# Cross-attention on one core: bias on ScalarE, V1 behind two energy tiles, second x behind y

## The chip, the cores and the metric

The kernel runs on one core of a Trainium2 chip. The metric is device time in microseconds (us), the median of several runs; lower is better. One further execution was taken by the hardware profiler, and all rows below come from it. Engines: TensorE (PE; its weight loads are PEld), VectorE (DVE), ScalarE (ACT), GpSimd (POOL) and SyncE (SP), which issues transfers.

## The reference

For each of 32 batches, x and y are 256 channels by 1024 positions (fp32), and the weights are 256 x 256:

```python
x_q = einsum('oc,bcn->bno', w_qk, y);  x_k = einsum('oc,bcn->bon', w_qk, x)
x_v = einsum('oc,bcn->bon', w_v, x) + b_v
attention = softmax(einsum('bnc,bcm->bnm', x_q, x_k), axis=-1)
attention = attention / (1e-07 + attention.sum(axis=1, keepdims=True))
x_r = einsum('bcn,bnm->bcm', x_v, attention)
return x + relu(einsum('oc,bcn->bon', w_t, x - x_r) + b_t)
```

## The kernel before

**Forms.** Each fp32 operand of a product is split into three forms (HIGH, REST, LOW), and a product is the sum of three products of forms. So every step of TensorE is 12 matmuls of 128x512 or a like number. The weights are multiplied together once: `gw` is w_qk's square, `vw` is w_t w_v, `tw` is w_t transposed. The bias of v goes through w_t as well: w_t times b_v is needed as `ubias` (times 1e-7), `nbias` (less b_t) and `xbias` (b_t less it).

**Tokens.** The order of TensorE is written out by hand in strings of tokens (lines 167 to 181): SET_UP, then FIRST for the first batch, STEADY for the next 29, BEFORE for the last but one and LAST for the last.

- `k0 k1`: keys, g = gw x, with the forms `gf` (one ScalarE operation and two VectorE operations of 1024 columns each).
- `V0 V1` (for the first batch's own, `v0` for the next batch's first half): values of one half of the positions (line 420). VectorE transposes PSUM into `turned`; four stores take `turned` to DRAM (`blocks`); one load brings it back, into `yr` for the first half and into `turned` for the second; ScalarE and GpSimd make the forms `uf`.
- `W0 W1`: w_t x, read from PSUM by ScalarE with `xbias` into `xe` (line 470).
- `E0`..`E7`: energy of 128 positions (line 478), then softmax: minimum on VectorE, exponential with its sum on ScalarE, reciprocal, and for each half of the columns VectorE's sum into `acc` and the forms `ef` (HIGH on ScalarE, REST on VectorE); LOW is made on ScalarE and GpSimd.
- `A0`..`A7` (in the last batch the eighth is cut into `a0 a1`): uf times ef, summed in PSUM over the eight. A0 to A3 need uf's first half, A4 to A7 the second.
- `S`: sums of attention over rows, on VectorE, giving `rc`. `O`: finish: (A + ubias) rc, plus xe, relu, plus x again, and the store. In the last batch `R`, `D`, `F`, `G` do this in another way: D1 divides in PSUM, F1 adds w_t x on top and stores, G0 does the other half of the channels.
- `X`: load the next batch's x and make its forms `xf` (line 359). `Y2 Y3`: load the next batch's y, one half of the positions each (line 327), into `yr` and then the forms `yf`; two of them are made by accumulating transfers on GpSimd's queue.
- In SET_UP `z` is a product of zeros that keeps TensorE busy, `G` and `H` are the halves of gw, `T` and `Q` the transposition of w_t and vw, `x0 x1` the forms of the first x, `fJkh` a piece of the first keys, `b` the bias (line 820), `y` both loads of the first y.

**PSUM.** There are four pairs of banks. A token with `^` takes turns on the pairs 3 and 2 (`upper`, line 863); the others take turns on 0 and 1. The A tokens sum in pairs 2 and 3. A token can start when the pair's earlier content has been read.

**The planner.** `Plan` (line 17) holds every operation with its engine, an assumed duration and lag, and the names it reads and writes. TensorE keeps the order of the tokens. The lists of the other engines, SP's and GpSimd's transfers among them, are made by list scheduling: of the operations that are ready, the one due first, where the due time is what its users leave less an optional `early`. The names only set the order; on the chip an operation waits for the data that it really touches.

The operations of the page all have line 231, the line of the helper that records them.

Of the kernel before, what the change touches and what calls it, by code (L numbers as in the profile page):

```python
# [9 lines left out]
F32 = mybir.dt.float32  # L10
F32R = mybir.dt.float32r
AF = mybir.ActivationFunctionType
ALU = mybir.AluOpType
AX = mybir.AxisListType


class Plan:
# [147 lines left out]


SET_UP = (
    "z z G H z x0 x1 fH00 z z z T fR00 b fL00 fH01 fR01 fL01 Q fH11 fR10 fL11 fL10 y fH10 fR11"
)
FIRST = (  # L170
    "V0^ V1^ W1^ E0 E1^ W0^ E2 X E3 A0 A1 E4 Y2 E5 A2 A3 E6 E7 A4 A5 S Y3 v0 A6 A7 O k0 k1"
)
STEADY = (
    "W0^ E0^ E1 E2 W1^ V1^ E3 Y2 A0 E4 A1 E5 A2 X E6 A3 E7 Y3 S A4 A5 v0 k1 A6 A7 k0 O"
)
BEFORE = (
    "V1^ E0 E1 W0^ W1^ E2 A0 E3 X A1 E4 A2 E5 A3 E6 Y2 E7 A4 Y3 A5 v0 k1 A6 k0 A7 S O"
)
LAST = (
    "E0 E1^ V1^ E2 E3 A0 A1 E4 E5 A2 A3 E6 E7 R1 A4 A5 S W0 A6 a0 a1 G0 D1 F1"  # L180
)


# [1 line left out]
def kernel(  # L185
# [13 lines left out]
    P = 128  # L199
    KC = C // P  # L200
# [4 lines left out]
    EPS = 1e-7  # L205
# [12 lines left out]
    one = ctx.enter_context(tc.tile_pool(name="one", bufs=1))  # L218
# [17 lines left out]
    pe, dve, act, pool, sync = (InOrder(g) for g in (nc.tensor, nc.vector, nc.scalar, nc.gpsimd, nc.sync))  # L236
    plan = Plan()


    def on_pe(count, columns, reads, writes, trace):  # L240
        plan.add("pe", count * max(columns / 2400 + 1 / 75, 1 / 9), 0.163, reads, writes, trace)

    def on_act(columns, reads, writes, trace, more=0.0):
        plan.add("act", columns / 1200 + 0.1 + more, 0.09, reads, writes, trace)

    def on_dve(columns, reads, writes, trace):
        plan.add("dve", columns / 960 + 0.16, 0.0, reads, writes, trace)

    def dve_in_sbuf(columns, reads, writes, trace):
        busy = columns / 960 + 0.07  # L250
# [5 lines left out]
    def on_pool(columns, reads, writes, trace):  # L256
        busy = columns * 2.25 / 1024 + 0.12
        plan.add("pool", busy, 0.0, reads, writes, trace, port=busy)

    def by_sync(landing, reads, writes, trace, early=0.0):  # L260
        plan.add("sync", 0.4, landing, reads, writes, trace, early=early)
# [4 lines left out]
    def by_pool(landing, reads, writes, trace):  # L266
        plan.add("pool", 1.2, landing, reads, writes, trace)

    def value(v):
        return v.bitcast(F32)  # L270

    def flat(p):
        return p.rearrange("p h m -> p (h m)")

    def accumulate(into, from_):
        pool.dma_start(into, from_, accum_op=ALU.add)
# [5 lines left out]
    ubias = const.tile([P, KC, 1], F32, name="ubias")  # L282
    xbias = const.tile([P, KC, 1], F32, name="xbias")
# [7 lines left out]
    xr = one.tile([P, KC, N], F32, name="xr")  # L291
    yr = one.tile([P, KC, MB], F32, name="yr")
    xo = one.tile([P, N], F32, name="xo")
    turned = one.tile([P, N], F32, name="turned")
    blocks = outside.tile([P, N], F32, name="blocks")
    xe = one.tile([P, KC, N], F32, name="xe")
    z = one.tile([P, KC, N], F32, name="z")
    acc = one.tile([P, N], F32, name="acc")
    rc = one.tile([P, N], F32, name="rc")
    small = one.tile([P, 3, NT, 1], F32, name="small")  # L300
    nbias = one.tile([P, KC, 1], F32, name="nbias")
    banks = ps_m.tile([P, 8, MB], F32, name="banks")

    def pair(j):
        return banks[:, 2 * j : 2 * j + 2]

    def in_pair(j):
        return [f"bank{2 * j}", f"bank{2 * j + 1}"]

    def matmul(into, lhs, rhs, start, stop):  # L310
        pe.matmul(into, lhs, rhs, start=start, stop=stop, skip_group_check=True)
# [44 lines left out]
    def x_names(j, k, halves=range(MH)):  # L356
        return [f"xf{j}{k}{h}" for h in halves]

    def load_x(b):
        for k in range(KC):  # L360

            def of(k=k):
                raw = [f"xr{k}{h}" for h in range(MH)]
                by_sync(5.0, [], raw, lambda: sync.dma_start(xr[:, k], x[b, ts(k, P)]))
                on_act(N, raw, x_names(HIGH, k), lambda: act.copy(xf[:, HIGH, k], xr[:, k]))
                on_pool(
                    N, raw + x_names(HIGH, k), x_names(REST, k),
                    lambda: pool.tensor_tensor(xf[:, REST, k], xr[:, k], value(xf[:, HIGH, k]), ALU.subtract),
                )
                on_act(  # L370
                    N, x_names(HIGH, k), x_names(LOW, k),
                    lambda: act.mul(xf[:, LOW, k], value(xf[:, HIGH, k]), 1.0 / UP),
                )
                by_pool(
                    8.2, x_names(LOW, k) + x_names(REST, k), x_names(LOW, k),
                    lambda: accumulate(value(xf[:, LOW, k]), value(xf[:, REST, k])),
                )

            of()
# [40 lines left out]
    def values(b, q, j_pair):  # L420

        both, at, u = pair(j_pair), in_pair(j_pair), uf[q]
        for i in range(KC):
            for j in ORDER:

                def of(i=i, j=j):
                    for k in range(KC):
                        matmul(
                            both[:, i], vw[:, j, k, ts(i, P)], xf[:, j, k, ts(q, MB)],
                            j == ORDER[0] and k == 0, j == ORDER[-1] and k == KC - 1,  # L430
                        )

                on_pe(KC, MB, [f"vw{j}{k}" for k in range(KC)] + [f"xf{j}{k}{q}" for k in range(KC)], [at[i]], of)
        on_dve(
            N, at, ["turned"],
            lambda: dve.transpose(
                turned.rearrange("p (a t i r) -> p i t a r", a=NG, t=HT, i=KC),
                both.rearrange("p i (t a r) -> p i t a r", t=HT, a=NG),
            ),
        )  # L440
        names = [f"uf{q}{j}" for j in range(FORMS)]

        def out_of():
            for g in range(NG):
                sync.dma_start(
                    blocks.rearrange("(a r) (g s) -> r g a s", a=NG, g=NG)[:, g],
                    turned[ts(g, G32)].rearrange("p (a s) -> p a s", a=NG),
                )

        plan.add("sync", 2.4, 3.0, ["turned"], ["blocks"], out_of)  # L450
        back, name = (turned, "turned") if q else (flat(yr), "yr")
        by_sync(4.5, ["blocks"], [name], lambda: sync.dma_start(back, blocks))

        def natural(v):
            return v.rearrange("p (t g s) -> p g t s", t=HT, g=NG)

        raw = back.rearrange("p (g t s) -> p g t s", t=HT, g=NG)
        high, low, rest = (natural(u[:, j]) for j in range(FORMS))
        on_act(N, [name], [names[HIGH]], lambda: act.copy(high, raw))
        on_pool(  # L460
            N, [name, names[HIGH]], [names[LOW]],
            lambda: pool.tensor_tensor(low, raw, value(high), ALU.subtract),
        )
        on_act(N, [names[LOW]], [names[LOW]], lambda: act.mul(u[:, LOW], value(u[:, LOW]), UP))
        on_pool(
            N, [name, names[LOW]], [names[REST]],
            lambda: pool.tensor_tensor(rest, raw, value(low), ALU.subtract),
        )
# [134 lines left out]
    def divided(c):  # L603

        for h in range(MH):

            def of(c=c, h=h):
                p = pair(2 + c)[:, h]
                on_dve(
                    MB, [in_pair(2 + c)[h], "rc", "bias"], [in_pair(2 + c)[h]],  # L610
                    lambda: dve.scalar_tensor_tensor(p, p, ubias[:, c], rc[:, ts(h, MB)], ALU.add, ALU.mult),
                )

            of()
# [69 lines left out]
    bt = two(3)[:, 0, P : P + KC].rearrange("p (k o) -> p k o", o=1)  # L684
# [135 lines left out]
    def biases():  # L820

        by_sync(5.6, [], ["bv"], lambda: sync.dma_start(bvs, b_v.partition_broadcast(P)), early=38.0)
        by_sync(
            5.4, [], ["bt"], lambda: sync.dma_start(bt, b_t.rearrange("(k p o) -> p k o", p=P, o=1)), early=36.0
        )
        each = two(0)
        on_pool(
            KC * C, ["wt0", "wt1", "bv", "z0", "z1"], ["wqk0", "wqk1"],
            lambda: pool.tensor_tensor(each, wt, bvs.unsqueeze(1).broadcast_to([P, KC, C]), ALU.mult),
        )  # L830

        def of():
            dve.tensor_reduce(nbias[:, :, 0], each, AX.X, ALU.add)
            dve.tensor_scalar(ubias[:, :, 0], nbias[:, :, 0], EPS, None, ALU.mult)
            dve.tensor_tensor(nbias[:, :, 0], nbias[:, :, 0], bt[:, :, 0], ALU.subtract)
            dve.tensor_scalar(xbias[:, :, 0], nbias[:, :, 0], -1.0, None, ALU.mult)

        plan.add("dve", 1.05, 0.0, ["wqk0", "wqk1", "bt", "z0", "z1"], ["bias"], of, port=1.05)

    def set_up(token):  # L840
        if token in ("G", "H"):
# [102 lines left out]
```

## Time and profile before

| | |
|---|---|
| median of 3 runs | 1937.35 us (1935.9 to 1937.73) |
| profiled execution | 1940.7 us, span of its instructions 1938.9 us |
| mean granted TensorE clock | 0.998 |
| TensorE matmul busy | 1928.4 us, 99% |
| TensorE weight load busy | 1595.3 us, 82% |
| VectorE, ScalarE, GpSimd busy | 77%, 76%, 80% |
| chain that ended last | TensorE 98%, VectorE 1% |

A row of a timeline has the start in us, the duration, the engine, the line, the operation, the tile written and those read, the shapes, and how many were merged; the bracket has the idle time of the engine ahead of it and what ended that. A row of windows has the stretch, its length, the busy time of PE, PEld, DVE, ACT and POOL with the number of instructions, the granted clock, the share of the DMA engines and GB/s. A row of groups has the count, then busy time, mean ns of one, and idle time ahead. Matmuls overlap in their records, so the pace is read from the starts.

### The profile page before, as it was taken

How to read it: one execution, taken by the hardware profiler on the slowest of the kernel's cores; microseconds unless marked ns; L12 is line 12 of the kernel's file. 1: busy time of each engine (PE TensorE's matmuls, PEld its weight loads, DVE VectorE, ACT ScalarE, POOL GpSimd, SP SyncE). 2: the span in 40 equal slices, each digit the busy share in tenths (PEclk: the TensorE clock that was granted, in tenths of full speed). 3: DMA queues.
4: the chain of work that ended last, by engine and by line, in shares of the span. 5: the costliest groups of instructions: out<-in, count | busy, mean ns of one | idle time of the engine just before them, and what ended most of it. 6: DMA issues, size and time to landing. Idle time of an engine off the chain costs nothing.

```text
span 1938.9 us, 24286 instructions
## 1 busy us (share of the span) xinstructions
PE 1928.4 (99%) x8494; PEld 1595.3 (82%) x8494; DVE 1499.1 (77%) x2109; ACT 1470.6 (76%) x1932; POOL 1553.9 (80%) x773
## 2 busy tenths in 40 slices
PE   8999999999999999999999999999999999999999
PEld 7888888888888888888888888888888888888887
DVE  6787777777777877778777787777787777877778
ACT  5779777787777877778877779777787777887776
POOL 4878878888778887788887878878888778887777
PEclk9999999999999999999999999999999999999999
DMA  6665666757666666666666665766756666666652
GB/s 182 142 162 153 178 154 137 166 153 181 162 143 151 159 170 168 147 145 168 163 165 155 147 163 152 181 156 138 164 151 178 163 145 149 161 170 169 156 106 76
DMA packets 128650, 301.88 MB, mean 156 GB/s; under 512 B 12688, under 2 KB 47120, under 8 KB 128528
## 3 DMA queue, kind: packets, MB, share of 16 engines
q1 hardware_dynamic: 92272, 200.45, 33.7%
q0 software_dynamic: 35680, 99.10, 29.0%
q8 instruction: 66, 1.08, 0.2%
q10 hardware_dynamic: 576, 0.79, 0.1%
q14 instruction: 56, 0.46, 0.1%
HBM read 167.38 MB, written 67.11 MB: 121 GB/s over the span
## 4 chain that ended last, share of the span: by engine, by line
PE 98%; DVE 1%; DMA 0%; ACT 0%; issue 0%; SPq 0%; DVEq 0%
PE banks L231 98%; DMA blocks<-turned 0%; DVE xf L231 0%; DVE nbias L231 0%; DVE z L231 0%; DVE turned L231 0%; DVE ef L231 0%; DVE parts L231 0%; DVE acc L231 0%; ACT ef L231 0%; DVE xbias L231 0%; DVE rc L231 0%; DVE banks L231 0%; DVE small L231 0%; SPq L231 0%
## 5 line engine op out<-in xcount | busy, mean ns | idle before, releaser
L231 PE MATMUL banks<-gf,yf 128*128 128x512 f32 x3072 | 729.6, 390 | 3.5 <-DVE turned L231 3.5
L231 POOL TENSOR_TENSOR ef<-ef 128x1024 fp32r<-128x1024 f32 x256 | 649.6, 2539 | 100.4 <-DVE acc L231 59.5
L231 PE MATMUL banks<-ef,uf 128*128 128x512 f32 x3072 | 727.0, 389 | 0.0
L231 PEld LDWEIGHTS banks<-gf,yf 128*128 128x128 f32 x3072 | 578.0, 188 | 124.3 <-DVE turned L231 3.9
L231 PEld LDWEIGHTS banks<-ef,uf 128*128 128x128 f32 x3072 | 576.6, 188 | 119.7
L231 DVE TENSOR_REDUCE small<-banks 128x1 f32<-128x1024 f32 x256 | 312.5, 1221 | 145.7 <-PE banks L231 145.7
L231 DVE SCALAR_TENSOR_TENSOR ef<-banks,small,ef 128x512 fp32r<-128x512 f32 x512 | 372.4, 743 | 56.5 <-ACT ef L231 55.4
L231 ACT ACTIVATE ef<-banks,small 128x512 fp32r<-128x512 f32 x512 | 336.4, 688 | 12.8 <-DVE acc L231 1.2
L231 ACT ACTIVATE banks<-banks,small 128x1024 f32<-128x1024 f32 x256 | 279.4, 1091 | 60.9 <-DVE small L231 60.6
L231 DVE SCALAR_TENSOR_TENSOR acc<-banks,small,acc 128x512 f32<-128x512 f32 x448 | 317.3, 744 | 5.6
L231 ACT ACTIVATE gf<-banks 128x1024 fp32r<-128x1024 f32 x64 | 65.8, 1030 | 315.9 <-PE banks L231 315.9
L231 ACT ACTIVATE ef<-ef 128x1024 fp32r<-128x1024 f32 x256 | 272.9, 1067 | 1.2
L231 POOL TENSOR_TENSOR z<-z,xe 128x1024 f32<-128x1024 f32 (+1 forms) x64 | 150.4, 2366 | 119.2 <-DVE z L231 116.8
L231 POOL TENSOR_TENSOR uf<-yr,uf 128x1024 fp32r<-128x1024 f32 x64 | 153.4, 2397 | 55.3 <-ACT uf L231 55.3
L231 PE MATMUL banks<-xf,tw 128*128 128x512 f32 x774 | 184.9, 388 | 2.1 <-DVE turned L231 1.2
L231 PE MATMUL banks<-xf,gw 128*128 128x512 f32 x768 | 185.3, 390 | 0.0
L231 PE MATMUL banks<-xf,vw 128*128 128x512 f32 x768 | 184.4, 389 | 0.0
L231 PEld LDWEIGHTS banks<-xf,tw 128*128 128x128 f32 x774 | 144.7, 188 | 32.9 <-DVE turned L231 1.6
L231 PEld LDWEIGHTS banks<-xf,vw 128*128 128x128 f32 x768 | 144.1, 188 | 30.2 <-DVE z L231 0.2
L231 PEld LDWEIGHTS banks<-xf,gw 128*128 128x128 f32 x768 | 143.8, 188 | 30.4 <-issue 0.4
L231 POOL TENSOR_TENSOR xf<-xr,xf 128x1024 fp32r<-128x1024 f32 x62 | 149.2, 2407 | 23.8 <-DVE turned L231 22.1
L231 POOL TENSOR_TENSOR uf<-turned,uf 128x1024 fp32r<-128x1024 f32 x64 | 156.2, 2441 | 0.3 <-ACT uf L231 0.3
(68 smaller groups left out, 1597.7 us busy)
## 6 DMA issues: line engine op xcount, KB each, us to landing
yr<-in_ctx_dram SPq DMA_DIRECT2D x64, 512.0 KB, 3.9
blocks<-turned SPq DMA_DIRECT2D x256, 128.0 KB, 3.0
yf<-in_ctx_dram POOLq DMA_DIRECT2D x63, 512.0 KB, 6.1
yf<-yf POOLq DMA_DIRECT2D x63, 512.0 KB, 7.1
xr<-in_x_dram SPq DMA_DIRECT2D x62, 512.0 KB, 3.6
xo<-in_x_dram SPq DMA_DIRECT2D x62, 512.0 KB, 4.4
xf<-xf POOLq DMA_DIRECT2D x62, 512.0 KB, 5.5
out_dram<-z SPq DMA_DIRECT2D x62, 512.0 KB, 4.5
```

Source lines behind the costliest of these rows:

```text
L231: self.last = getattr(self.engine, name)(*args, **kwargs)
```

## The change

The biases' reduction stays on VectorE, into a tile of its own; the three operations behind it become four on ScalarE. The token strings change except STEADY's, the planner is told of another lag for the first batch's stores to `blocks`, of an earlier due time for D's operations, and of a need of `yr` for the load of the second batch's x.

```diff
 SET_UP = (
-    "z z G H z x0 x1 fH00 z z z T fR00 b fL00 fH01 fR01 fL01 Q fH11 fR10 fL11 fL10 y fH10 fR11"
+    "x1 z z z G z x0 z H fH00 fH01 b z fR00 T fL00 fR01 Q fL01 fR11 fR10 fL11 fH11 y fH10 fL10"
 )
 FIRST = (
-    "V0^ V1^ W1^ E0 E1^ W0^ E2 X E3 A0 A1 E4 Y2 E5 A2 A3 E6 E7 A4 A5 S Y3 v0 A6 A7 O k0 k1"
+    "V0^ W1^ E0^ E1 V1^ E2^ W0^ E3 A0 X A1 E4 E5 A2 A3 Y2 E6 E7 Y3 A4 A5 k1 v0 A6 A7 S O k0"
 )
...
 BEFORE = (
-    "V1^ E0 E1 W0^ W1^ E2 A0 E3 X A1 E4 A2 E5 A3 E6 Y2 E7 A4 Y3 A5 v0 k1 A6 k0 A7 S O"
+    "V1^ E0 W0^ E1 W1^ X E2 A0 E3 A1 E4 A2 E5 A3 E6 E7 Y2 A4 Y3 A5 v0 k0 k1 A6 S A7 O"
 )
 LAST = (
-    "E0 E1^ V1^ E2 E3 A0 A1 E4 E5 A2 A3 E6 E7 R1 A4 A5 S W0 A6 a0 a1 G0 D1 F1"
+    "E0 E1^ V1^ E2 E3 A0 A1 E4 E5 A2 A3 E6 R1 E7 A4 A5 W0 A6 a0 S a1 D1 F1 G0"
 )
...
-    def on_dve(columns, reads, writes, trace):
-        plan.add("dve", columns / 960 + 0.16, 0.0, reads, writes, trace)
+    def on_dve(columns, reads, writes, trace, early=0.0):
+        plan.add("dve", columns / 960 + 0.16, 0.0, reads, writes, trace, early=early)
...
+    wtb = one.tile([P, KC, 1], F32, name="wtb")
...
-                by_sync(5.0, [], raw, lambda: sync.dma_start(xr[:, k], x[b, ts(k, P)]))
+                by_sync(5.0, ["yr"] if b == 1 else [], raw, lambda: sync.dma_start(xr[:, k], x[b, ts(k, P)]))
...
-        plan.add("sync", 2.4, 3.0, ["turned"], ["blocks"], out_of)
+        plan.add("sync", 2.4, 3.0 if b else 5.0, ["turned"], ["blocks"], out_of)
...
                     lambda: dve.scalar_tensor_tensor(p, p, ubias[:, c], rc[:, ts(h, MB)], ALU.add, ALU.mult),
+                    early=3.0 + 2 * h,
...
+        plan.add(
+            "dve", 0.68, 0.0, ["wqk0", "wqk1", "z0", "z1"], ["wtb"],
+            lambda: dve.tensor_reduce(wtb[:, :, 0], each, AX.X, ALU.add),
+        )
+
         def of():
-            dve.tensor_reduce(nbias[:, :, 0], each, AX.X, ALU.add)
-            dve.tensor_scalar(ubias[:, :, 0], nbias[:, :, 0], EPS, None, ALU.mult)
-            dve.tensor_tensor(nbias[:, :, 0], nbias[:, :, 0], bt[:, :, 0], ALU.subtract)
-            dve.tensor_scalar(xbias[:, :, 0], nbias[:, :, 0], -1.0, None, ALU.mult)
+            for c in range(KC):
+                act.activation(xbias[:, c], wtb[:, c], AF.Identity, bias=bt[:, c], scale=-1.0)
+            act.mul(ubias[:, :, 0], wtb[:, :, 0], EPS)
+            act.mul(nbias[:, :, 0], xbias[:, :, 0], -1.0)
 
-        plan.add("dve", 1.05, 0.0, ["wqk0", "wqk1", "bt", "z0", "z1"], ["bias"], of, port=1.05)
+        plan.add("act", 0.85, 0.09, ["wtb", "bt", "z1"], ["bias"], of)
```

## The prediction

> **What bounds the kernel now.** I read first the list of who waited for whom, for TensorE alone (total, times, longest), then the timeline of TensorE in the first 60 us, then that of all engines in the first 50 us.
>
> ```profile
> PE banks L231 <- DVE turned L231: 4.6, 2, 3.5
> PE banks L231 <- DVE few L231: 1.1, 1, 1.1
> PE banks L231 <- DVE banks L231: 1.0, 1, 1.0
> ```
>
> These are all of TensorE's waits in the whole span. Outside the start and the last microseconds it never waits, so the change can win only there, and lose anywhere.
>
> ```profile
> 1.05 2.93 PE L231 MATMUL banks<-few 128*128 128x128 f32 x12 [1.05 <-DVE few L231]
> ...
> 16.06 5.61 PE L231 MATMUL banks<-xf,vw 128*128 128x512 f32 x24
> 22.82 3.04 PE L231 MATMUL banks<-xf,tw 128*128 128x512 f32 x12 [1.15 <-DVE turned L231]
> 25.69 2.88 PE L231 MATMUL banks<-gf,yf 128*128 128x512 f32 x12
> 32.02 5.49 PE L231 MATMUL banks<-gf,yf 128*128 128x512 f32 x12 [3.45 <-DVE turned L231]
> 37.31 3.10 PE L231 MATMUL banks<-xf,tw 128*128 128x512 f32 x12
> 40.25 5.60 PE L231 MATMUL banks<-gf,yf 128*128 128x512 f32 x24
> 45.69 5.60 PE L231 MATMUL banks<-ef,uf 128*128 128x512 f32 x24
> ```
>
> The rows are V0 V1, W1, E0, E1, W0, E2 E3, A0 A1. From 40.25 to 45.69 two tokens take 5.44, so one (12 matmuls) takes 2.72. From V0's start to A0's start stand eight tokens, 21.76, and they took 45.69 - 16.06 = 29.63. **7.87 us are lost there**: 1.32 ahead of W1, 3.76 ahead of E1, 2.57 inside E1 (5.29 instead of 2.72), 0.22 inside W0. The loss inside E1 is the clock (PEclk, the column behind the engines):
>
> ```profile
> 30.00:32.00 2.00, 0.00 (x0) 0.00 (x0) 1.28 (x2) 0.00 (x0) 0.00 (x0) 0.71 0.50 78
> 32.00:34.00 2.00, 1.98 (x5) 1.59 (x6) 1.08 (x1) 0.89 (x1) 0.00 (x0) 0.50 0.60 240
> ```
>
> The wait of 3.45 halved it; the 1.15 ahead of W1 cost no clock, for W1 and E0 follow at the usual pace. Why both waited, from the timeline of all engines:
>
> ```profile
> 8.90 4.45 SPq L231 DMA_DIRECT2D xr<-in_x_dram  x2
> ...
> 16.01 0.67 DVE L231 TENSOR_REDUCE nbias<-z 128x2 f32<-128x512 f32 x1
> ...
> 16.58 1.92 ACT L231 ACTIVATE gf<-banks 128x1024 fp32r<-128x1024 f32 x2
> 16.72 0.17 DVE L231 TENSOR_SCALAR ubias<-nbias 128x2 f32<-128x2 f32 x1
> 16.92 2.26 DVE L231 TENSOR_TENSOR nbias<-nbias,z 128x2 f32<-128x2 f32 x1
> 17.40 1.75 POOL L231 TENSOR_TENSOR tw<-acc,tw 128x512 fp32r<-128x512 f32 x1
> ...
> 19.16 1.29 POOL L231 TENSOR_TENSOR yf<-yf 128x512 fp32r<-128x512 f32 x1
> 19.22 1.26 DVE L231 TENSOR_SCALAR xbias<-nbias 128x2 f32<-128x2 f32 x1
> 20.39 1.21 DVE L231 SCALAR_TENSOR_TENSOR gf<-gf,banks 128x1024 fp32r<-128x1024 f32 x1
> ...
> 21.52 1.24 DVE L231 STREAM_TRANSPOSE turned<-banks 128x1024 f32<-128x1024 f32 x1
> ...
> 22.79 1.79 SPq L231 DMA_DIRECT2D blocks<-turned  x4
> ...
> 30.72 1.25 DVE L231 STREAM_TRANSPOSE turned<-banks 128x1024 f32<-128x1024 f32 x1 [4.46 <-DMA blocks<-turned]
> 30.80 0.34 SPq L231 DMA_DIRECT2D yr<-blocks  x1
> ```
>
> W1 takes the pair that V0 had, so it waits for V0's transpose, which stands behind the bias operations and a key form on VectorE. E1^ takes V1's pair, and V1's transpose waits until the four stores of the first have left `turned`.
>
> **The change part by part.**
>
> *Bias on ScalarE.* VectorE loses ubias, nbias and xbias: from 16.72 to 20.48, 3.76 us. Two of them are long because of GpSimd: 2.26 ends at 19.18 with GpSimd's operation that ends at 19.15, and 1.26 at 20.48 with one that ends at 20.45. The reduction stays, 0.67. ScalarE gains four operations on one or two columns; the nearest row is its copy of one column:
>
> ```profile
> 3.92 0.19 ACT L231 COPY acc<-few 128x1 f32<-128x1 f32 x1
> ```
>
> 4 x 0.19 = 0.76. They wait for the reduction, and behind them on ScalarE stand the casts of y; their first user is the reading of W1 at 21.5 (below). Behind gf they cost nothing, ahead of gf up to 0.76; I take 0. If the reduction meets GpSimd's 1.75, VectorE is free at 18.44 instead of 16.69, against 17.60 when gf's first half is there: up to 0.84, taken 0.
> [...]
>
> *Start-up order.* One more idle product stands ahead of G: 2 of 12 records of 2.93, 0.49. It may be given back before the keys end, for TensorE is filled with idle products there. Between -0.5 and +0.5; I take 0.3 and add it at the end.
>
> *FIRST.* The order is V0 W1 E0 E1 V1 E2 W0 E3 A0; the pairs taken are 3, 2, 3, 0, 2, 3, 2, 1. W1 waits for nobody: V0 16.06 to 18.78, W1 to 21.50. Now **E0** waits for V0's transpose and for gf, with E1 and V1 behind it. VectorE has four operations of 1.20 (row 20.39) and one of 1.24 from 17.60 (16.58 plus half of 1.92, and a little): done at 23.64. E0 comes to its last form at 21.50 + 4/6 x 2.72 = 23.31: loss 0.33. E0 to 24.55, E1 to 27.27, V1 to 29.99. **E2** takes E0's pair, with W0, E3 and A0 behind it. A row of softmax, from the page's groups:
>
> ```profile
> L231 DVE TENSOR_REDUCE small<-banks 128x1 f32<-128x1024 f32 x256 | 312.5, 1221 | 145.7 <-PE banks L231 145.7
> L231 DVE SCALAR_TENSOR_TENSOR ef<-banks,small,ef 128x512 fp32r<-128x512 f32 x512 | 372.4, 743 | 56.5 <-ACT ef L231 55.4
> L231 ACT ACTIVATE banks<-banks,small 128x1024 f32<-128x1024 f32 x256 | 279.4, 1091 | 60.9 <-DVE small L231 60.6
> ```
>
> From 24.75: 1.22, 1.09, two operations on one column (0.19 and 0.17 by the rows above, with the hand-overs about 0.5), four halves of 0.743 on VectorE: 30.5, its first half 1.5 earlier. E2 begins at 29.99 with the first half: loss 0. E2 also needs y's second half of columns, whose last transfer was issued at 24.07:
>
> ```profile
> 24.07 1.25 POOL L231 DMA_DIRECT2D yf<-yf  x1
> ```
> ```profile
> yf<-yf POOLq DMA_DIRECT2D x1, 256.0 KB, 7.7
> ```
>
> 24.07 + 7.7 = 31.8, and E2 needs it at 29.99 + 0.91 = 30.9: loss 0.9 if it stays there. *x's move* answers to that: the two loads of 8.90 (1 MB), which ran beside y's first piece, go behind the reading back of V0's blocks on SP's queue (the planner's name yr was last written there). V1's four stores queue behind them, due only with uf's second half. I take 0, with 0.9 as the bound. **W0** at 32.71 waits for V1's transpose: `turned` is free when V0's stores land. V0's transpose ends by 21.2, 1.6 earlier than in the trace, so 30.7 becomes 29.1; VectorE has room at 30.5, done 31.7: loss 0. E3 from 35.43 to 38.15. **A0** then needs uf's first half (its second form at 38.15 + 0.91 = 39.06). Its chain after reading back:
>
> ```profile
> 34.22 1.04 ACT L231 CAST uf<-yr 128x1024 fp32r<-128x1024 f32 x1
> ...
> 35.34 2.36 POOL L231 TENSOR_TENSOR uf<-yr,uf 128x1024 fp32r<-128x1024 f32 x1 [10.02 <-ACT uf L231]
> ...
> 41.05 1.07 ACT L231 ACTIVATE uf<-uf 128x1024 fp32r<-128x1024 f32 x1
> ...
> 42.21 2.40 POOL L231 TENSOR_TENSOR uf<-yr,uf 128x1024 fp32r<-128x1024 f32 x1 [3.67 <-ACT uf L231]
> ```
>
> From the transpose's end (22.76) to 44.61 these were 21.85, of which 3.35 (37.70 to 41.05) lay on ScalarE behind E1's late softmax. Without these, 21.2 + 18.50 = 39.7; loss 0.64. A softmax sum on GpSimd (2.5 us) may step between: 0 to 2.5, I take 0.5. So A0 runs as if started at 39.3, with the start-up 39.6, taken as 39.7. **45.69 - 39.7 = 6.0 us won.**
>
> *BEFORE and LAST.* TensorE's order loses nothing today, so k0 ahead of A6 and the loads moved by a token can only lose; they are covered by the same 2.72 per token, and I take 0. At the end D1 goes ahead of G0:
>
> ```profile
> 1930.52 1.41 DVE L231 SCALAR_TENSOR_TENSOR banks<-banks,ubias,rc 128x512 f32<-128x512 f32 x2
> ...
> 1931.98 3.08 PE L231 MATMUL banks<-xf,tw 128*128 128x256 f32 x18 [0.97 <-DVE banks L231]
> ```
>
> a1's last matmul lets D1's second half begin about 1931.05, 0.13 earlier; G0 behind it may end up to 0.5 later than F1. -0.1 to +0.5, taken 0.
>
> Sum: the profiled execution took 1940.7 (span 1938.9); it becomes 1934.7. The median of the runs is 3.35 lower, 1937.35; less the same 6.0 it is **1931.4**.
>
> **The rivals.**
>
> *The wait moves to A0* (0.16). ScalarE's 3.35 stays in uf's chain: 43.0, a wait of 3.9 inside A0. Gain 45.69 - (43.0 - 0.91) = 3.6, 1933.8; if the clock halves as it did behind 3.45, 2.79 more are lost, 1936.6. For it: an engine takes its list in order, and E1's and E2's softmax fall into the same time. Against: E1 is no longer held by V1, so its softmax is early. Middle 1935.2. [...]
>
> *Slower: the other pair in every batch* (0.08). FIRST now has six ^ instead of five, so in STEADY W0 takes the pair that `finish` frees second:
>
> ```profile
> 203.22 2.48 DVE L231 SCALAR_TENSOR_TENSOR z<-banks,ubias,rc 128x1024 f32<-128x1024 f32 x2 [1.45 <-PE banks L231]
> ```
> ```profile
> 206.20 2.88 PE L231 MATMUL banks<-xf,tw 128*128 128x512 f32 x12
> ```
>
> The second ends at 205.70, W0 starts at 206.20: 0.50 of slack. If VectorE is late there by more than 0.50 + 6.0/30 = 0.70, thirty batches eat the gain; at 0.83 they cost 9.9, so 1941.3. Against: VectorE idles 1.45 ahead of it.
>
> *The change doesn't do what it says* (0.05): V0's stores land no earlier, `turned` is free at 30.7, and with queueing on VectorE W0 waits 1 to 3 us: gain 3 to 5, 1933.4.
>
> *VectorE's gain is only what the operations cost undisturbed* (0.03): 3 x 0.17, and GpSimd holds up others instead. VectorE is then done with gf at about 25.9, 2.3 later, and so is uf: gain 3.7, 1933.7. [...]
>
> **How the numbers follow.** The forecast has 0.68, its own range 1929.3 (no loss at all and 0.5 won at the start: 8.0) to 1932.9 (gain 4.5, with 0.9, 0.84 or a sum on GpSimd against it). The range reaches over half of the first rival, to 1935.6. About 0.2% or 3.9 us is what a measurement can tell from no change: faster 0.68 + 0.03 (of the third rival) = 0.71; within it 0.16 + 0.02 + 0.03 = 0.21; slower 0.08.
>
> **What would show it.** Right: no wait of TensorE for `turned` over 1 us, a clock of 1.00 from 16 to 45 us, VectorE's first gf by 18 us, A0 between 38 and 40.5 us, and TensorE without waits from there to the last 7 us. Wrong: a wait of 3 us or more in E2, W0 or A0; idle time ahead of W0 in each batch; ScalarE's four operations ahead of gf; a last stretch from a1 on longer by more than 0.5 us.

## The result, and the profile after

| | before | after |
|---|---|---|
| median | 1939.53 us of 20 runs (1935.42 to 1941.7) | 1942.89 us of 20 runs (1937.19 to 1943.74) |
| profiled execution | 1940.7 us, span 1938.9 us | 1943.16 us, span 1941.4 us |

The ratio is 1.0013 [1.0007, 1.0019]: no change by the bound of 0.2%, with an interval that lies above 1. The forecast of 1931.4 and its range up to 1935.6 were wrong.

TensorE's waits after, from the list of who waited for whom (total, times, longest). The waits for `turned` are gone, as forecast. Those for `parts` at the start and for `banks` at the end stand where before had 1.1 and 1.0; those for `xf`, `ef` and `gw` are new, and the forecast didn't have them:

```profile
PE banks L231 <- DVE xf L231: 2.6, 2, 1.9
PE banks L231 <- DVE ef L231: 2.4, 5, 0.9
PE banks L231 <- DVE parts L231: 1.1, 1, 1.1
PE banks L231 <- DVE banks L231: 0.9, 1, 0.9
PE banks L231 <- DVE gw L231: 0.8, 1, 0.8
```

The timeline of TensorE after, with its start, the first batch, batch 2 and the end:

```profile
13.32 0.73 PE L231 MATMUL banks<-xf,gw 128*128 128x512 f32 x2 [0.81 <-DVE gw L231]
14.68 0.73 PE L231 MATMUL banks<-xf,gw 128*128 128x512 f32 x2 [0.62 <-DVE xf L231]
17.36 3.75 PE L231 MATMUL banks<-xf,gw 128*128 128x512 f32 x8 [1.95 <-DVE xf L231]
20.91 3.68 PE L231 MATMUL banks<-xf,vw 128*128 128x512 f32 x12
24.42 2.88 PE L231 MATMUL banks<-xf,tw 128*128 128x512 f32 x12
...
50.23 5.60 PE L231 MATMUL banks<-gf,yf 128*128 128x512 f32 x24
...
160.12 3.06 PE L231 MATMUL banks<-xf,vw 128*128 128x512 f32 x12 [0.79 <-DVE ef L231]
...
1858.82 1.66 PE L231 MATMUL banks<-gf,yf 128*128 128x512 f32 x6 [0.90 <-DVE ef L231]
1860.70 4.38 PE L231 MATMUL banks<-gf,yf 128*128 128x512 f32 x18 [0.22 <-DVE ef L231]
...
1934.06 3.08 PE L231 MATMUL banks<-xf,tw 128*128 128x256 f32 x18 [0.85 <-DVE banks L231]
```

The reader compares starts. V0 begins at 20.91; before it began at 16.06: **+4.85** ahead of everything that the forecast counted. From V0 to E4 it takes 50.23 - 20.91 = 29.32; before, A0 began at 45.69 and two tokens of 2.72 later E4, at 51.13, which is 35.07: **-5.75**, close to the 6.0. So the first batch gave about what was forecast (it would have been 0.8 more, had V0 itself not run at a lower clock, below), and the start-up took it back. What is left, -0.90, is lost in batch 2 (0.79 ahead of V1, and with smaller ones the kernel is 0.53 behind at 206) and in the last but one batch (1.69 more in E6 and E7, at 1858.82 and 1860.70). F1, the last product, begins at 1934.06 instead of 1931.98.

Why the start-up is long is seen by laying VectorE's timeline beside GpSimd's. The third column on is engine, line, operation, output and inputs:

```profile
8.60 0.68 DVE L231 TENSOR_TENSOR xf<-xr,xf 128x512 fp32r<-128x512 f32 x1
...
9.54 1.71 DVE L231 SCALAR_TENSOR_TENSOR xf<-xf 128x512 fp32r<-128x512 f32 x1
11.17 1.76 DVE L231 TENSOR_TENSOR xf<-xr,xf 128x512 fp32r<-128x512 f32 x1
12.86 0.41 DVE L231 SCALAR_TENSOR_TENSOR gw<-banks,gw 128x256 fp32r<-128x256 f32 x1
13.19 1.43 DVE L231 TENSOR_TENSOR xf<-xr,xf 128x512 fp32r<-128x512 f32 x1
14.54 2.67 DVE L231 SCALAR_TENSOR_TENSOR xf<-xf 128x512 fp32r<-128x512 f32 x1
```
```profile
9.41 1.29 POOL L231 TENSOR_TENSOR z<-z 128x512 f32<-128x512 f32 x1 [8.09 <-PE banks L231]
10.89 1.49 POOL L231 TENSOR_TENSOR xe<-acc,tw 128x512 f32<-128x512 f32 x1 [0.20 <-ACT tw L231]
12.68 1.40 POOL L231 TENSOR_TENSOR yf<-yr,yf 128x512 fp32r<-128x512 f32 x1 [0.29 <-ACT yf L231]
...
14.95 1.70 POOL L231 TENSOR_TENSOR tw<-acc,tw 128x512 fp32r<-128x512 f32 x1
```

An operation on x takes 0.68 alone. The four that meet an operation of GpSimd end at 11.25, 12.93, 14.62 and 17.21, GpSimd's four at 10.70, 12.38, 14.08 and 16.65: each time 0.54 to 0.56 later. They lose 1.03, 1.08, 0.75 and 1.99, together 4.85. (That V0 is late by the same figure is a coincidence, as the sum below shows.) The operation of 0.41 at 12.86, which reads one of its operands from PSUM, runs at its usual pace beside GpSimd's third. Before, the same work of GpSimd fell mostly behind x:

```profile
9.85 3.13 DVE L231 TENSOR_TENSOR xf<-xr,xf 128x512 fp32r<-128x512 f32 x2
12.90 0.41 DVE L231 SCALAR_TENSOR_TENSOR gw<-banks,gw 128x256 fp32r<-128x256 f32 x1
13.24 1.28 DVE L231 SCALAR_TENSOR_TENSOR xf<-xf 128x512 fp32r<-128x512 f32 x2
```

It lost 3.13 - 1.36 = 1.77 there. The difference is 3.08. The rest is the clock, in the windows of after (length, busy time of PE, PEld, DVE, ACT, POOL, then PEclk):

```profile
14.00:16.00 2.00, 0.78 (x3) 0.30 (x2) 2.00 (x2) 0.00 (x0) 2.00 (x3) 0.93 0.40 59
16.00:18.00 2.00, 0.64 (x2) 0.58 (x3) 2.00 (x3) 0.42 (x2) 0.65 (x1) 0.50 0.88 235
18.00:20.00 2.00, 2.00 (x6) 1.57 (x5) 1.83 (x5) 1.45 (x3) 1.29 (x1) 0.50 1.09 312
20.00:22.00 2.00, 2.00 (x6) 1.55 (x5) 0.23 (x1) 1.28 (x2) 0.00 (x0) 0.50 0.32 50
22.00:24.00 2.00, 2.00 (x9) 1.57 (x9) 0.99 (x1) 2.00 (x6) 1.21 (x1) 0.87 0.12 17
```

At 0.50 the eight key matmuls take 20.91 - 17.36 = 3.55 instead of 8/12 x 2.72 = 1.81: 1.74 more, and 3.08 + 1.74 = 4.82 of the 4.85, if all of VectorE's loss is taken as lying on the path. The mean of 0.93 from 14 to 16 says that the clock fell at about 15.7, which is 0.3 us into the wait that began at 15.41.

Not every run pays for the clock. In after's 20 runs, 17 have a mean clock of 0.998 or 0.999 and take 1940.52 to 1943.74; three have 1.000 and take 1937.19, 1937.21 and 1937.56. Before has the same spread: of 34 runs that were made beside the first four experiments, those under 1937.8 all have 1.000 and those over 1939.6 all have 0.998 or 0.999. The two groups of before stay where they are in the three sets of its runs below (34, 33 and 15): at 1.000 their medians are 1937.28, 1937.15 and 1936.81, under it 1940.34, 1940.21 and 1940.31. What differs is how many are under it: 19, 11 and 9. So the median of all runs moves with that share, and it is worth reading a kernel by its groups too.

### The profile page after: what moved, and what is told of

It reads as the page before. It is cut to its first block, busy times and chain, and to the rows that moved or that the text cites. A ratio compares the mean times of both kernels' runs of the same rounds, so it can differ in the third digit from the quotient of the medians.

```text
span 1941.4 us, 24339 instructions
## 1 busy us (share of the span) xinstructions
PE 1929.5 (99%) x8494; PEld 1594.0 (82%) x8494; DVE 1498.0 (77%) x2106; ACT 1464.0 (75%) x1936; POOL 1550.0 (80%) x773
## 3 DMA queue, kind: packets, MB, share of 16 engines
q8 instruction: 66, 1.08, 0.2%
## 4 chain that ended last, share of the span: by engine, by line
PE 97%; DVE 1%; ACT 0%; DMA 0%; POOL 0%; SPq 0%; issue 0%; POOLq 0%; ACTq 0%
PE banks L231 97%; DVE xf L231 0%; DMA yr<-blocks 0%; DVE small L231 0%; SPq L231 0%; DVE ef L231 0%; DVE acc L231 0%; DVE z L231 0%; DMA blocks<-turned 0%; POOL uf L231 0%; ACT banks L231 0%; POOL ef L231 0%; DVE banks L231 0%; ACT ef L231 0%; DVE turned L231 0%
## 5 line engine op out<-in xcount | busy, mean ns | idle before, releaser
L231 POOL TENSOR_TENSOR ef<-ef 128x1024 fp32r<-128x1024 f32 x256 | 630.4, 2464 | 91.3 <-ACT ef L231 47.1
L231 DVE SCALAR_TENSOR_TENSOR ef<-banks,small,ef 128x512 fp32r<-128x512 f32 x512 | 360.8, 741 | 9.7 <-ACT ef L231 6.6
L231 ACT ACTIVATE ef<-banks,small 128x512 fp32r<-128x512 f32 x512 | 329.7, 700 | 10.1 <-DVE acc L231 10.0
L231 POOL TENSOR_TENSOR uf<-turned,uf 128x1024 fp32r<-128x1024 f32 x64 | 168.4, 2631 | 0.0
L231 DVE RECIPROCAL small<-small 128x1 f32<-128x1 f32 x256 | 41.4, 162 | 163.6 <-ACT banks L231 163.5
```

The costliest lines, as they stand in the source:

```text
L231: self.last = getattr(self.engine, name)(*args, **kwargs)
```

## The experiments

The theory (A): the new SET_UP puts GpSimd's operations among VectorE's on x; TensorE waits, its clock halves; the rest of the change gains about what was forecast, less a little in BEFORE and LAST. The rivals (B) put the loss elsewhere: in the first batch itself, in the load of x, or in the last batches. Before's own median was 1939.53 beside after, 1938.72 beside the first four experiments, 1937.47 beside the next four and 1938.69 beside the last, so across these sets a kernel is read by its ratio, or by its median less before's median of the same set; for after that is 1942.89 - 1939.53 = +3.36.

One thing about the planner bears on how far an edit reaches. It makes four plans of the other engines' lists and keeps the one that is shortest by its own count (`LOOKS` and `best`). By the plans that the sources make, the changed kernel keeps the first, with 1933.66 us against 1933.92 for the third; before, and every kernel below with the old SET_UP or with the old BEFORE and LAST, keeps the third. So undoing either in the changed kernel also gives VectorE, ScalarE and GpSimd other lists in every batch. Two pairs don't have this: SET_UP alone changes with BEFORE and LAST old (the lists differ up to 24 us only), and BEFORE and LAST alone change with SET_UP old (the lists differ from 1822 us on only).

**Undo the start-up order.** The changed kernel with SET_UP as before:

```diff
-    "x1 z z z G z x0 z H fH00 fH01 b z fR00 T fL00 fR01 Q fL01 fR11 fR10 fL11 fH11 y fH10 fL10"
+    "z z G H z x0 x1 fH00 z z z T fR00 b fL00 fH01 fR01 fL01 Q fH11 fR10 fL11 fL10 y fH10 fR11"
```

> The changed kernel with SET_UP's tokens as before. Theory A (the new start-up order puts four of VectorE's operations on x behind GpSimd's, TensorE waits for them and its clock halves): V0 starts at 16 to 16.6 us instead of 20.91, no wait of TensorE between 10 and 17 us, and the time is 4 to 5 us under the changed kernel's, about 1938 where that has 1943. Rival B (the late keys come from the bias on ScalarE or from x's later load): V0 stays at 20 or later and the time within 1 us of the changed kernel's.

Measured: 1935.88 (1934.15 to 1937.59, 11 runs) against before's 1938.72 (34 runs), ratio 0.9982 [0.9974, 0.9991]; clock 1.000 in all runs. V0 begins at 16.12 and E4 at 45.40:

```profile
16.12 2.88 PE L231 MATMUL banks<-xf,vw 128*128 128x512 f32 x12
```

Against before that is -2.84, so undoing one string moves the median by 3.36 + 2.84 = 6.2 us, and the intervals of the two ratios lie apart. It is more than the 4.85 of the profile's V0; the other plan can have a part in it, and the pair without that is read below.

**Undo the end.** The changed kernel with BEFORE and LAST as before:

```diff
-    "V1^ E0 W0^ E1 W1^ X E2 A0 E3 A1 E4 A2 E5 A3 E6 E7 Y2 A4 Y3 A5 v0 k0 k1 A6 S A7 O"
+    "V1^ E0 E1 W0^ W1^ E2 A0 E3 X A1 E4 A2 E5 A3 E6 Y2 E7 A4 Y3 A5 v0 k1 A6 k0 A7 S O"
...
-    "E0 E1^ V1^ E2 E3 A0 A1 E4 E5 A2 A3 E6 R1 E7 A4 A5 W0 A6 a0 S a1 D1 F1 G0"
+    "E0 E1^ V1^ E2 E3 A0 A1 E4 E5 A2 A3 E6 E7 R1 A4 A5 S W0 A6 a0 a1 G0 D1 F1"
```

> The changed kernel with BEFORE and LAST as before. Theory A (the wait of 0.90 and 0.22 for ef at 1859 us belongs to the new order of the last two batches): it goes, and the span is 1.7 to 2.1 us under the changed kernel's 1941.4. Rival B (it is handed on from the first batch, by the turned order of the pairs): it stays, and the time is within 0.5 us of the changed kernel's.

Measured: 1941.22 (1934.84 to 1942.81, 12 runs), ratio 1.0006 [0.9996, 1.0016]; against before +2.50, 0.9 less than after, with overlapping intervals. Its span of 1939.4 is 2.0 less. The waits at 1858.82 and 1860.70 are gone, and the one of batch 2 too. Two of its runs have a clock of 1.000 and take 1934.84 and 1936.14. Its start-up, with the lists of the other plan, shows the collision in a worse form; VectorE, GpSimd and TensorE, from the timeline of this kernel:

```profile
15.05 5.33 DVE L231 SCALAR_TENSOR_TENSOR xf<-xf 128x512 fp32r<-128x512 f32 x1
...
15.67 1.72 POOL L231 TENSOR_TENSOR yf<-yr,yf 128x512 fp32r<-128x512 f32 x1
16.91 1.70 POOL L231 TENSOR_TENSOR tw<-acc,tw 128x512 fp32r<-128x512 f32 x1
18.13 1.69 POOL L231 TENSOR_TENSOR yf<-yf 128x512 fp32r<-128x512 f32 x1
...
20.43 1.22 PE L231 MATMUL banks<-xf,gw 128*128 128x512 f32 x2 [4.20 <-DVE xf L231]
```

One operation of 0.68 takes 5.33, behind three of GpSimd in a row, and ends 0.56 after the third (20.38 against 19.82). By its record it began ahead of the first.

**FIRST alone, and FIRST with the bias.** The first of the two is the kernel before with the new FIRST, the new lag and the new need of the load of x; the second is the changed kernel with SET_UP, BEFORE and LAST as before, so it has the bias on ScalarE as well. The first's edit of before:

```diff
-    "V0^ V1^ W1^ E0 E1^ W0^ E2 X E3 A0 A1 E4 Y2 E5 A2 A3 E6 E7 A4 A5 S Y3 v0 A6 A7 O k0 k1"
+    "V0^ W1^ E0^ E1 V1^ E2^ W0^ E3 A0 X A1 E4 E5 A2 A3 Y2 E6 E7 Y3 A4 A5 k1 v0 A6 A7 S O k0"
...
-                by_sync(5.0, [], raw, lambda: sync.dma_start(xr[:, k], x[b, ts(k, P)]))
+                by_sync(5.0, ["yr"] if b == 1 else [], raw, lambda: sync.dma_start(xr[:, k], x[b, ts(k, P)]))
...
-        plan.add("sync", 2.4, 3.0, ["turned"], ["blocks"], out_of)
+        plan.add("sync", 2.4, 3.0 if b else 5.0, ["turned"], ["blocks"], out_of)
```

> The kernel before with FIRST's new tokens, the lag of 5.0 and x behind yr; the bias stays on VectorE, SET_UP, BEFORE and LAST are as before. Theory A (moving V1 behind E0 and E1 carries the gain, as 5.75 us from V0 to E4 in the changed kernel say): V0 at 16.1, E4 between 45 and 47, time 4 to 6 us under before. Rival B (without the 3.76 us freed on VectorE, E0 waits for gf until about 26 and uf is late): V0 at 16.1, E4 at 48 or later, time less than 3 us under before.

> The changed kernel with SET_UP, BEFORE and LAST as before, so the bias on ScalarE, FIRST, the lag, x behind yr and D's due time alone. Theory A: V0 at 16.1 to 16.6, E4 at 45.4 to 46, none of the later losses but perhaps batch 2's 1.3: 4 to 6 us under before, about 1934 where before has 1939. Rival B (a gain in the first batch is always given back later because the lists of the other engines are made for other times): E4 as early, but at least 3 us of waits of TensorE behind it, and less than 2 us under before.

Measured: FIRST alone 1937.27 (1936.21 to 1940.42, 11 runs), ratio 0.999 [0.9981, 0.9998], E4 at 47.90. With the bias 1935.65 (1934.0 to 1936.72, 10 runs), ratio 0.9982 [0.9973, 0.999], E4 at 44.83, span 1933.1, clock 1.000 in all runs. FIRST alone has the waits that the bias on VectorE leaves, from its timeline of TensorE:

```profile
22.96 2.65 PE L231 MATMUL banks<-gf,yf 128*128 128x512 f32 x9 [1.07 <-DVE turned L231]
26.24 3.69 PE L231 MATMUL banks<-gf,yf 128*128 128x512 f32 x15 [0.63 <-DVE gf L231]
```

These are E0 and E1 behind V0's transpose and the forms of the keys, so FIRST alone came out as its rival B had it, nearly. With the bias on ScalarE both are gone, from the timeline of the other:

```profile
16.05 2.89 PE L231 MATMUL banks<-xf,vw 128*128 128x512 f32 x12
18.78 2.99 PE L231 MATMUL banks<-xf,tw 128*128 128x512 f32 x12
21.60 5.74 PE L231 MATMUL banks<-gf,yf 128*128 128x512 f32 x24
27.18 2.88 PE L231 MATMUL banks<-xf,vw 128*128 128x512 f32 x12
29.90 2.93 PE L231 MATMUL banks<-gf,yf 128*128 128x512 f32 x12
...
39.84 5.15 PE L231 MATMUL banks<-ef,uf 128*128 128x512 f32 x21 [0.40 <-DVE ef L231]
44.83 5.61 PE L231 MATMUL banks<-gf,yf 128*128 128x512 f32 x24
```

The median says 1.45 us for FIRST alone and 3.07 for both, so 1.6 for the bias. The profile of the second lies where the prediction put it, and the median does not: the gain of 3.07 is half of the 6.0. The groups say what it is made of. All ten runs of the second have 1.000; they lie 1.63 under before's 15 runs with 1.000 in this set (1937.28) and 4.69 under its other 19 (1940.34). FIRST alone has 1937.25 in its ten runs with 1.000, and so gains nothing against the former: its 1.45 is the clock. Beside the kernel of "Undo the end" the second differs by SET_UP alone, and lies 1941.22 - 1935.65 = 5.57 under it (where 10 of the 12 runs are under 1.000). That is the price of the new SET_UP without the other plan.

**Keep TensorE busy in the new start-up.** The changed kernel with 14 idle products into a pair that is free, between the keys' pieces:

```diff
-    "... fL00 fR01 Q fL01 fR11 fR10 fL11 fH11 y fH10 fL10"
+    "... fL00 fR01 Q fL01 q3 fR11 q3 fR10 q8 fL11 fH11 y fH10 fL10"
...
+    def keep_busy(count, bank):
+        plan.add(
+            "pe", 0.0, 0.0, ["few"], [f"bank{bank}"],
+            lambda: [pe.matmul(banks[:, bank, :P], few, few, start=True, stop=True) for _ in range(count)],
+        )
```

> The changed kernel with 14 more idle products where TensorE waits in the start-up (3 ahead of fR11, 3 ahead of fR10, 8 ahead of fL11), in a pair that nobody reads then; the lists of the other engines are the same. Theory A (the waits let the clock halve, and that is a second loss beside them): the clock stays at 1.00 to 28 us, V0 takes 2.72 instead of 3.51, and the median falls by 2 to 5 us, to the three fast-clocked runs of the changed kernel at 1937.2 to 1937.6. Rival B (the clock's part is small, the runs differ by something else): median within 1 us of the changed kernel's 1943, runs still spread over 1937 to 1943.

Measured: 1940.38 (1938.5 to 1941.09, 11 runs), ratio 1.0008 [0.9999, 1.0017] against before's 1937.47 (33 runs). In the windows of this kernel the clock stays at 1.00 where after had 0.50, and TensorE's timeline has V0 still late:

```profile
16.00:18.00 2.00, 1.91 (x11) 1.31 (x10) 2.00 (x1) 0.58 (x2) 2.00 (x3) 1.00 0.89 173
```
```profile
19.19 0.73 PE L231 MATMUL banks<-xf,gw 128*128 128x512 f32 x2 [1.28 <-DVE xf L231]
19.85 3.03 PE L231 MATMUL banks<-xf,vw 128*128 128x512 f32 x12
```

Against before it is +2.91, which is no gain that can be told from after's +3.36; but the spread is 2.6 us instead of 6.6. The products take away the runs over 1941.1 and the ones under 1938.5 alike. So the clock alone is not the loss: with it at 1.00, V0 still begins at 19.85, 3.79 late, and one operation of VectorE took 3.60 here. By groups the two parts can be estimated, from medians of different sets: after's 17 runs under 1.000 have 1942.99, the ten with 1.000 here 1940.40, and before's 22 with 1.000 in this set 1937.15. That is about 2.6 for the clock and 3.2 for what VectorE loses. That after's three runs with a clock of 1.000 were shorter than any of these suggests that VectorE met GpSimd less in them; only profiled runs have a timeline, so this is argued and not shown.

**Take GpSimd out of VectorE's way.** The changed kernel with three operations of GpSimd in the start-up cut to 32 of 512 columns each, so most of the sum for the bias and of the lower forms of `tw` is left out. Two fills of zeros on VectorE near 1 us stand in for what isn't written; otherwise the lists of all engines stay as they are:

```diff
-            lambda: pool.tensor_tensor(d, wtT, value(high), ALU.subtract),
+            lambda: pool.tensor_tensor(d[:, :32], wtT[:, :32], value(high)[:, :32], ALU.subtract),
...
-            lambda: pool.tensor_tensor(rest, wtT, value(low), ALU.subtract),
+            lambda: pool.tensor_tensor(rest[:, :32], wtT[:, :32], value(low)[:, :32], ALU.subtract),
...
-            lambda: pool.tensor_tensor(each, wt, bvs.unsqueeze(1).broadcast_to([P, KC, C]), ALU.mult),
+            lambda: pool.tensor_tensor(each[:, :, :16], wt[:, :, :16], bvs.unsqueeze(1).broadcast_to([P, KC, C])[:, :, :16], ALU.mult),
```

> The changed kernel with three of GpSimd's start-up operations (the bias product and both differences for tw) cut from 512 to 32 columns, so the forms of w_t and the bias are partly left out; two fills of zeros on VectorE at 1 us stand in for what is not written. All lists keep their order. Theory A (VectorE's operations with both operands in SBUF wait for GpSimd's): the ones that took 1.71, 1.76 and 2.67 us take 0.7, the one of 1.43 beside y's difference stays, V0 starts by 17.5 at a clock of 1.00, and the time is 4.5 to 6.5 us under the changed kernel's 1943. Rival B (the new order of VectorE's own operations or ScalarE's casts make the keys late): V0 at 19 or later, time within 2 us of the changed kernel's.

Measured: 1936.73 (1935.7 to 1938.2, 11 runs), ratio 0.9994 [0.9985, 1.0003], clock 1.000; V0 at 15.63, E4 at 44.92. From its timelines, VectorE's four operations of above, and V0:

```profile
9.29 0.68 DVE L231 SCALAR_TENSOR_TENSOR xf<-xf 128x512 fp32r<-128x512 f32 x1
9.89 0.69 DVE L231 TENSOR_TENSOR xf<-xr,xf 128x512 fp32r<-128x512 f32 x1
...
10.89 0.68 DVE L231 TENSOR_TENSOR xf<-xr,xf 128x512 fp32r<-128x512 f32 x1
11.49 0.74 DVE L231 SCALAR_TENSOR_TENSOR xf<-xf 128x512 fp32r<-128x512 f32 x1
...
15.63 3.18 PE L231 MATMUL banks<-xf,vw 128*128 128x512 f32 x12 [0.20 <-DVE vw L231]
```

They take 0.68 to 0.74, and against before the median is at -0.74, 4.1 us lower than after's (4.5 to 6.5 were expected), with intervals that lie apart and the order of SET_UP untouched. This shows that the new order loses its time through GpSimd's operations, and not by itself. The third operation was expected to stay at 1.43 beside GpSimd's work on y; that work came later here, at 13.58, behind it, so one of the four meetings (0.75) went for another reason.

**The load of the second x.** The changed kernel with the load not behind y, then the same edit on the best kernel so far (bias and FIRST new, the rest as before):

```diff
-                by_sync(5.0, ["yr"] if b == 1 else [], raw, lambda: sync.dma_start(xr[:, k], x[b, ts(k, P)]))
+                by_sync(5.0, [], raw, lambda: sync.dma_start(xr[:, k], x[b, ts(k, P)]))
```

> The changed kernel without the need of yr, so the second batch's x is loaded at about 9 to 13 us again, beside y's first piece; only SP's list differs. Theory A (the order of tokens puts VectorE behind GpSimd, whatever x does): V0 within 1 us of 20.9 and the time within 1 us of the changed kernel's. Rival B (x's later load lets y land earlier, so GpSimd's difference for y falls among VectorE's operations on x, 12.68 instead of 14.51): y's cast at 13 or later, V0 at 18.5 or earlier, and the time 2 us or more under the changed kernel's.

> The kernel with the bias on ScalarE and FIRST's new tokens, SET_UP, BEFORE and LAST as before, and the second batch's x loaded early again (no need of yr); only SP's list differs from the run with x late (1935.65 us). Theory A (x's later load is worth nothing in itself; in the changed kernel it did harm, because y's operations on GpSimd came earlier among VectorE's): the same within 1 us, V0 at 16.1, E2 without a wait for yf. Rival B (y's second half of columns would then land at 31.8, past E2's need at 30.9): a wait of TensorE in E2 of about 1 us, and the time 1 to 2 us over.

Measured: on the changed kernel 1938.39 (1937.11 to 1942.86, 11 runs), ratio 1.0012 [1.0003, 1.0021]; six of its runs lie at 1937.11 to 1938.39 with a clock of 1.000, five at 1940.73 and over. Its profile has V0 at 16.37: GpSimd's operation on y comes later than in after:

```profile
13.80 1.30 POOL L231 TENSOR_TENSOR yf<-yr,yf 128x512 fp32r<-128x512 f32 x1 [0.50 <-ACT yf L231]
```

After had it at 12.68. Of VectorE's operations on x only the last meets it here:

```profile
14.12 1.53 DVE L231 SCALAR_TENSOR_TENSOR xf<-xf 128x512 fp32r<-128x512 f32 x1
```

Rival B says that x's later load lets y in earlier. From the issue of y's first load to ScalarE's cast, which waited for it, it took 12.68 - 7.56 = 5.12 here, and with x late 11.85 - 7.66 = 4.19 (idle products) and 12.45 - 8.26 = 4.19 (small GpSimd operations): 0.93 more with x beside it. But the place of y's operation varies as much with x late: 12.68 in after, 13.00 with the idle products and 13.58 with the small GpSimd operations, whose lists are after's but for the edit. So one profile doesn't show that x's load moved it. The times don't settle it either: the median is +0.92 against before's, 2.4 less than after's +3.36, with 6 of 11 runs in the lower group instead of 3 of 20, but the ratio lies within after's interval. On the best kernel the load is worth nothing: 1935.12 (1934.33 to 1937.36, 11 runs), ratio 0.9981 [0.9972, 0.999], against 0.9982 with it, and E2 waits for no y in either. It has the lowest median of the study, which can't be told from that of the kernel with x late.

**Idle products in the kernel before.** Twelve idle products between E0 and E1, made by the same `keep_busy`, fill the wait of 3.45 in which the clock of before fell:

```diff
-    "V0^ V1^ W1^ E0 E1^ W0^ E2 X E3 A0 A1 E4 Y2 E5 A2 A3 E6 E7 A4 A5 S Y3 v0 A6 A7 O k0 k1"
+    "V0^ V1^ W1^ E0 q E1^ W0^ E2 X E3 A0 A1 E4 Y2 E5 A2 A3 E6 E7 A4 A5 S Y3 v0 A6 A7 O k0 k1"
```

> The kernel before with 12 idle products between E0 and E1, in a pair that is free then; the lists of the other engines are the same. Theory A (in about half of its runs the wait of 3.45 ahead of E1 halves the clock, in the others not, and that is the spread from 1935.2 to 1943.0): no run over 1938.5, clock 1.000 in all, median 1936 to 1937, 2 to 3 us under before. Rival B (the spread has another cause): the same spread and median as before, within 1 us.

Measured: 1937.59 (11 runs) against before's 1937.47 (33 runs), ratio 1.0002 [0.9993, 1.0011]. One of the 11 took 3972.78, for a reason that isn't known, and without it the median is 1937.42; of the other ten, nine have a clock of 1.000 and lie at 1936.66 to 1938.81, and one has 0.998 and takes 1943.84. From its timeline of TensorE:

```profile
31.00 3.00 PE L231 MATMUL banks<-gf,yf 128*128 128x512 f32 x12
...
47.44 5.60 PE L231 MATMUL banks<-gf,yf 128*128 128x512 f32 x24
```

E4 begins at 47.44 instead of 51.13; 1.02 of this is that E1 begins at 31.00 instead of 32.02, and 2.67 that it runs at the full clock. The products leave one run of ten in the upper group instead of 11 of 33, and do not lower the median, because most of before's runs in that set were in the lower group already. Theory A had no run over 1938.5 and 2 to 3 us in the median; neither came.

## Why the prediction was wrong, point by point

- **Start-up order, "Between -0.5 and +0.5; I take 0.3": the step that failed.** It counted an idle product alone. It was costed on TensorE alone, with the idle products as cover; the cover of the first forms of x is VectorE, and what VectorE takes hangs on GpSimd (0.68 alone, 1.43 to 2.67 beside it in after). It measured +4.85 in the profile, and 5.57 in the median (1935.65 to 1941.22, the two kernels that differ by SET_UP alone). The rows of 2.26 and 1.26 had been read as "because of GpSimd" just above, and were used for the bias only. The planner doesn't warn either, though it has a rule for this meeting (`port`): by its plans V0 begins at 14.73 before and at 15.05 in the changed kernel, 0.3 later. The moved tokens issue operations on GpSimd too (`b`, `T`, `y`), and their place among VectorE's was not asked.
- **"The median ... less the same 6.0".** The 6.0 was right for the profiled execution: the kernel with bias and FIRST alone has a span of 1933.1, where 1938.9 - 6.0 = 1932.9 was forecast. But that execution was one of those whose clock fell, which the prediction itself had at 2.57 in E1 and 0.22 in W0, and 43 of before's 82 runs in the three sets have a clock of 1.000 and don't have this loss to win back. Against those of its set the kernel gains 1.63, against the others 4.69, and by the medians 3.07, 0.9982 [0.9973, 0.999]. Less the 2.79 of the clock the 6.0 would have been 3.2, so about half of that is still missing; where it goes stays open, since only profiled runs have a timeline. That the median of three lay 3.35 under the profiled time was seen and put down to nothing.
- **BEFORE and LAST, "can only lose ... I take 0".** E6 and E7 of the last but one batch lose 1.69 in the profile. The energy tiles wait for VectorE's `ef`; that the other engines' lists are the reason is argued, not shown. Undoing both strings takes 2.0 off the span and 0.9 off the median, but brings the other plan. In the pair without that, with the old SET_UP, the new strings have a wait of 1.03 for GpSimd's `ef` at 1893.28 instead, and the medians are 1935.88 and 1935.65: 0.2. Neither difference of medians can be told from nothing. Of D1 ahead of G0 nothing came: with LAST and D's due time old or new, all engines' lists are the same.
- **Batch 2, not in the prediction.** 0.79 ahead of V1 in after, and not with the old BEFORE and LAST, where the planner keeps the other plan. ScalarE's list has uf's cast ahead of E0's exponential, and the cast waits 3.79 us for its load; before has the same order there and a wait of 2.07. So that order alone is not the reason, and why the load comes later stays open.
- **FIRST and the bias: right.** V1 was forecast for 27.27 and began at 27.18, E2 for 29.99 and 29.90; A0 as if at 39.3 puts E4 at 44.74, and it began at 44.83. ScalarE's four bias operations took 0.48 for two, 0.20 and 0.20, behind gf.
- **x's move, taken 0.** Right by itself (1935.12 and 1935.65, ratios 0.9981 and 0.9982). Whether it moves y's operation of GpSimd into VectorE's way with the new SET_UP stays open.
- **The rivals.** *The wait moves to A0*: its pieces wait 0.21 and 0.40 in the kernel that has FIRST without the lost start-up; refuted. *The other pair in every batch*: after runs 0.53 behind before at 206 and 0.51 at 1855, so 27 batches cost nothing; refuted. *The change doesn't do what it says*: no wait for `turned` is left; refuted. *GpSimd holds up others instead* named the mechanism, at 0.03, and looked for it behind the keys instead of ahead of them; there VectorE did gain, with its first gf at 17.61 instead of 20.39 in the kernel of FIRST and the bias.

## What to carry to other kernels

An order that moves tokens moves operations on every engine that they issue on: lay the lists of VectorE and GpSimd side by side for each moved token, and price their meeting from the rows that show it. A gain that is read in one profiled execution counts for the median only if that execution's clock and time are those of the median run; with two groups of runs, sum for each. When a change of several strings comes out at nothing, undo them one at a time: here the bias and FIRST gain 3.07, and SET_UP loses 5.57. Where a planner makes the lists, see first that the undone string leaves the other lists as they are.

## What the runs showed of the hardware

- An operation of VectorE on x (128x512, its operands in SBUF) that was held behind one of GpSimd ended 0.54 to 0.57 us after it, in the start-ups of after, of the old start-up order, of the old end, of the idle products and of x early: 0.68 became 1.43 to 2.67 beside one, 3.60 beside two (idle products) and 5.33 beside three (the old end). Being passed over like this isn't the rule: with x early GpSimd's operation at 11.57 follows one that ends at 11.61, and VectorE's came through between them (10.73 to 12.16). Nor was every one held that overlapped: with the idle products the one at 9.52 kept its 0.68 beside GpSimd's of 9.49, which took 1.84. The operation that reads PSUM kept its 0.41 in after, and V0's transpose out of PSUM its 1.25 beside GpSimd's two from 17.40 to 20.46 (bias and FIRST). So did the biases' reduction, which reads one operand from SBUF: 0.68 at 16.81 beside GpSimd's from 15.96 to 17.71 (x early).
- The clock fell to 0.50 within a wait, after different times. In after it fell at about 15.7, 0.3 us into the third of three waits (0.81, 0.62 and 1.95); before at about 30.8, 2.3 us into the wait of 3.45 (0.71 in the row of 30 to 32). With the old end it was down by the end of the wait of 4.20: the two key matmuls behind it take 21.45 - 20.43 = 1.02 instead of 0.45, V0 25.12 - 21.45 = 3.67 instead of 2.72, and the mean from 20 to 100 is 0.98. In FIRST alone waits of 1.07 and 0.63 left it at 1.00. The longest wait of after's start-up was 1.95, and in 17 of its 20 runs the mean clock was under 1.000. With fourteen idle products in these gaps it was 1.000 in 10 of 11.
- The same kernel with the same lists comes out in two groups according to that clock (after 1937.19 to 1937.56 and 1940.52 to 1943.74; before by medians 3.1 to 3.5 us apart), so a removed wait shows in the spread as well as in the median: 2.6 us instead of 6.6 with the idle products in the new start-up.
